# Two graph attention layers per graph: head outputs kept feature-major, score rows sent through DRAM

## The chip, the cores, the metric

One core of a Trainium2 chip runs the whole program: 32 graphs, one after the other, in one launch. The metric is device time in microseconds (us), the median over executions. Two kernels that are compared in rounds ran on the same chip.

In the profile PE is TensorE, PEld its weight load, DVE VectorE, ACT ScalarE, POOL GpSimd, SP the engine that only issues DMAs. SBUF is the large on-chip memory, PSUM the small one that TensorE writes into.

## The reference, cut to what matters

```python
def reference(x, adj, ...):            # x (32, 512, 512), adj (32, 512, 512)
    h = maximum(layernorm(x), 0)
    x = x + L0(h, adj)                 # one attention over the neighbours, values = h
    h = maximum(layernorm(x), 0)
    return x + L1(adj, h)              # two GAT layers: 4 heads x 256 features with elu, then 1 head x 512

# an attention, with s the sources and d the destinations:
#   e[s, d] = leaky_relu(a[s] + c[d], 0.2);  -inf where there is no edge
#   out[d]  = sum_s softmax_s(e)[s, d] * value[s]
```

A graph has three kinds of attention: layer 0, the four heads of the first GAT layer (layer 1 below), and the second GAT layer (layer 2). Both kernels compute E[s, d] = exp(leaky(a[s] + c[d]) - m[d]) with s on the partitions, m[d] being leaky(c[d] + the largest a[s] over d's neighbours). With p = c - m and q = 0.2 c - m this is exp(max(a + p, 0.2 a + q)). So three rows must lie on all 128 partitions: a for the maxima, p and q for the weights.

## The kernel before: the parts that matter

```python
def spread(col_of):                    # a value per node -> a row on all partitions, IN PSUM
    row = p_bc.tile([P, N], F32, tag="bc", name="row")
    for t in range(T):
        nc.tensor.transpose(row[:, node_block(t)], col_of(t).to_broadcast([P, P]), ident)
    return row

def neighbour_max(amax, h, mask, row):             # 4 instructions on VectorE
    ... nc.vector.tensor_tensor_reduce(junk, mask[:, t, :], row, 1.0, LOWEST, ALU.add, ALU.max, accum_out=...)

def edge_weights(E, pq, h, a_of, a2_of, mask):
    p_row = spread(...); q_row = spread(...)
    for t in range(T):
        nc.scalar.activation(q, q_row, AF.Identity, bias=a2_of(t), scale=1.0)                    # ScalarE
        nc.vector.scalar_tensor_tensor(u, p_row, a_of(t), q, op0=ALU.add, op1=ALU.max)           # VectorE: "u"
        nc.gpsimd.tensor_add(u, u, mask[:, t, :])                                                # GpSimd: mask add
        nc.scalar.activation(E[:, t, :], u, AF.Exp)                                              # ScalarE

def inverse_sums(E):                   # 16 matmuls with a column of ones
    ...
# ... (cut) a head: acc[d, f] = E^T x values, one column of ones behind the 256 features for the sum;
# normalise, add bias, elu on VectorE; then eight TensorE transposes to get the feature-major h1T.
# Masks are transposed by TensorE. TensorE's order is left to the scheduler.
```

## Time and profile before

| | before |
|---|---|
| median of 3 runs | 5194.93 us (5193.39 to 5204.31) |
| TensorE busy, records | 96%, 20,224 |
| VectorE, ScalarE, GpSimd busy | 45%, 34%, 21% |
| granted TensorE clock, mean | 0.931 |
| one graph, from one graph's hn transposes to the next's | 160.3 us |

The prediction below shows the lines behind this table. This is from the page of the kernel before; the columns are line, engine, operation, output<-inputs, shapes, count | busy us in all, mean ns of one | idle time before them:

```profile
L204 POOL TENSOR_TENSOR u<-u,m 128x512 f32<-128x512 f32 x640 | 737.8, 1180 | 1844.2 <-DVE u L203 1803.7
...
L203 DVE SCALAR_TENSOR_TENSOR u<-row,ac,q 128x512 f32<-128x512 f32 x640 | 447.5, 745 | 747.5 <-ACT q L201 746.1
...
L180 DVE CUSTOM_DVE_ANT_0 junk_m<-m1T,row 128x512 bf16<-128x512 bf16 x640 | 394.4, 683 | 124.9 <-PE row L165 124.9
```

The mask add takes 1180 ns, u 745 ns, a masked maximum 683 ns. In u and in the maximum one input (`row`) is in PSUM.

### The profile page before, as it was taken

The page shows a single profiled execution, that of the slowest core. Times are in us where ns is not written, and L with a number is a line of the kernel's source. Part 1 is how long each engine was busy: PE and PEld are TensorE (multiplying, and loading weights), DVE is VectorE, ACT ScalarE, POOL GpSimd, SP SyncE. Part 2 cuts the span into 40 slices and gives each one's busy share as a digit, 9 for nine tenths or more (in the row PEclk, how much of TensorE's full clock was granted, in tenths as well). Part 3 has the DMA queues.
Part 4 walks back from the last instruction along what each step waited for, and adds up shares of the span by engine and source line. Part 5 has one row for each costly group of instructions (what it writes and reads, how often), then busy time and mean ns, then how long its engine had stood idle before and what let it go on. Part 6 is the DMA issues. An engine that isn't in the chain of part 4 may idle for free.

```text
span 5205.4 us, 52686 instructions
## 1 busy us (share of the span) xinstructions
PE 5003.1 (96%) x20224; PEld 3228.5 (62%) x20224; DVE 2326.8 (45%) x6180; ACT 1794.5 (34%) x2945; POOL 1108.0 (21%) x998
## 2 busy tenths in 40 slices
PE   6999999999999999999999999999999999999999
PEld 3666656666566666666665666656666666666565
DVE  5454434454444544345443444444454434544343
ACT  2333323433224333233332333322433323333232
POOL 1222211222112212122221222211221212222121
PEclk8899999999999999999999999999999999999999
DMA  2000000000000000000000000000000000000000
GB/s 103 20 13 17 25 25 25 9 17 25 25 25 9 17 25 25 25 17 17 17 25 25 25 9 17 25 25 25 9 17 25 25 25 17 17 17 25 9 9 9
DMA packets 53802, 111.11 MB, mean 21 GB/s; under 512 B 1840, under 2 KB 1840, under 8 KB 53552
## 3 DMA queue, kind: packets, MB, share of 16 engines
q1 hardware_dynamic: 50688, 100.67, 5.5%
q10 hardware_dynamic: 2864, 7.08, 0.4%
q8 instruction: 160, 2.62, 0.2%
q14 instruction: 90, 0.74, 0.0%
HBM read 74.19 MB, written 33.55 MB: 21 GB/s over the span
## 4 chain that ended last, share of the span: by engine, by line
PE 86%; POOL 5%; DVE 5%; ACT 3%; issue 1%; DMA 1%; DVEq 0%; POOLq 0%; ACTq 0%; SPq 0%
PE acc L222 31%; PE acc L399 18%; PE acc L333 17%; PE ps_c L309 8%; POOL u L204 5%; PE row L165 4%; PE pt L173 3%; PE ps L212 3%; DVE u L203 3%; ACT q L201 2%; ACT E L205 1%; DVE v L367 1%; DMA x<-in_x_dram 0%; DVE junk L126 0%; DMA adj<-in_adj_dram 0%
## 5 line engine op out<-in xcount | busy, mean ns | idle before, releaser
L222 PE MATMUL acc<-xl,E 128*128 128x257 f32 (+1 forms) x5120 | 1548.6, 453 | 67.2 <-ACT E L205 62.1
L222 PEld LDWEIGHTS acc<-xl,E 128*128 128x128 f32 x5120 | 996.0, 203 | 470.4 <-issue 258.1
L204 POOL TENSOR_TENSOR u<-u,m 128x512 f32<-128x512 f32 x640 | 737.8, 1180 | 1844.2 <-DVE u L203 1803.7
L399 PE MATMUL acc<-w_s,h1T 128*128 128x512 f32 x2048 | 952.9, 619 | 0.0
L333 PE MATMUL acc<-w_s,hT 128*128 128x512 f32 x2048 | 917.3, 604 | 0.0
L203 DVE SCALAR_TENSOR_TENSOR u<-row,ac,q 128x512 f32<-128x512 f32 x640 | 447.5, 745 | 747.5 <-ACT q L201 746.1
L333 PEld LDWEIGHTS acc<-w_s,hT 128*128 128x128 f32 x2048 | 392.1, 196 | 449.8 <-issue 449.8
L399 PEld LDWEIGHTS acc<-w_s,h1T 128*128 128x128 f32 x2048 | 397.9, 201 | 436.7 <-issue 436.7
L201 ACT ACTIVATE q<-row,a 128x512 f32<-128x512 f32 x768 | 478.9, 682 | 535.2 <-PE row L165 428.4
L338 ACT COPY xl<-acc 128x512 f32<-128x512 f32 x256 | 150.1, 586 | 1340.7 <-PE acc L333 1340.7
L205 ACT ACTIVATE E<-u 128x512 f32<-128x512 f32 x768 | 484.2, 630 | 222.2 <-POOL u L204 221.2
L222 PE MATMUL acc<-h,E 128*128 128x512 f32 x1024 | 453.8, 601 | 6.0 <-DVE x L284 6.0
L180 DVE CUSTOM_DVE_ANT_0 junk_m<-m1T,row 128x512 bf16<-128x512 bf16 x640 | 394.4, 683 | 124.9 <-PE row L165 124.9
L309 PEld LDWEIGHTS ps_c<-wa,h1T 128*128 128x128 f32 x2048 | 335.4, 257 | 50.2 <-PE pt L173 34.1
L309 PE MATMUL ps_c<-wa,h1T 128*128 128x2 f32 x2048 | 333.1, 295 | 28.1 <-DVE r L216 28.1
L222 PEld LDWEIGHTS acc<-h,E 128*128 128x128 f32 x1024 | 194.7, 193 | 238.2 <-issue 224.1
L174 ACT COPY h1T<-pt 128x512 f32<-128x512 f32 x256 | 138.8, 581 | 551.3 <-PE pt L173 551.3
L411 DVE SCALAR_TENSOR_TENSOR x<-acc,r,x 128x512 f32<-128x512 f32 x128 | 96.1, 751 | 401.5 <-PE acc L222 401.5
L165 PE MATMUL row<-ident,pq 128*128 128x128 f32 x1536 | 210.6, 277 | 62.7 <-ACT q L201 53.3
L212 PEld LDWEIGHTS ps<-ones,E 128*128 128x128 f32 x2048 | 258.9, 198 | 11.2 <-ACT E L205 5.4
L212 PE MATMUL ps<-ones,E 128*128 128x1 f32 x2048 | 246.6, 246 | 4.4 <-ACT E L205 4.4
L165 PEld LDWEIGHTS row<-ident,pq 128*128 128x128 f32 x1536 | 175.3, 139 | 120.4 <-ACT q L201 71.1
(71 smaller groups left out, 3727.8 us busy)
## 6 DMA issues: line engine op xcount, KB each, us to landing
adj<-in_adj_dram SPq DMA_DIRECT2D x32, 1024.0 KB, 5.1
x<-in_x_dram SPq DMA_DIRECT2D x32, 1024.0 KB, 5.1
out_dram<-x SPq DMA_DIRECT2D x32, 1024.0 KB, 4.2
w_s<-in_L_gnn_W_dram ACTq DMA_DIRECT2D x2, 2048.0 KB, 21.1
b_r<-in_L_gnn_b_dram ACTq DMA_DIRECT2D x1, 512.0 KB, 11.2
a_r<-in_L_gnn_att_src_dram ACTq DMA_DIRECT2D x1, 512.0 KB, 5.4
a_r<-in_L_gnn_att_dst_dram ACTq DMA_DIRECT2D x1, 512.0 KB, 4.0
ws_r<-in_L_gnn_attn_w_src_dram ACTq DMA_DIRECT2D x1, 256.0 KB, 5.2
```

Of the source, the lines that this page charges most:

```text
L165: nc.tensor.transpose(row[:, node_block(t)], col_of(t).to_broadcast([P, P]), ident)
L173: nc.tensor.transpose(pt[:, node_block(t)], src(t, k), identity)
L180: nc.vector.tensor_tensor_reduce(junk, mask[:, t, :], row, 1.0, LOWEST, ALU.add, ALU.max, accum_out=amax[:, t, h : h + 1])
L201: nc.scalar.activation(q, q_row, AF.Identity, bias=a2_of(t), scale=1.0)
L203: nc.vector.scalar_tensor_tensor(u, p_row, a_of(t), q, op0=ALU.add, op1=ALU.max)
L204: nc.gpsimd.tensor_add(u, u, mask[:, t, :])
L205: nc.scalar.activation(E[:, t, :], u, AF.Exp)
L212: nc.tensor.matmul(ps[:, t : t + 1], E[:, s, node_block(t)], ones, start=(s == 0), stop=(s == T - 1))
L222: nc.tensor.matmul(acc[:, :width], E[:, s, node_block(t)], values(s), start=(s == 0), stop=(s == T - 1))
L309: nc.tensor.matmul(ps[:, t, :], src[:, k, node_block(t)], wa[:, k, :], start=(k == 0), stop=(k == kn - 1))
L333: nc.tensor.matmul(acc, hT[:, k, node_block(t)], w1_s[:, k, half * 512 : (half + 1) * 512], start=(k == 0), stop=(k == KD - 1),)
L399: nc.tensor.matmul(acc, h1T[:, k, node_block(t)], w2_s[:, k, :], start=(k == 0), stop=(k == KH - 1))
```

## The change

The intent is to take work from TensorE, which bounds the kernel. The heads are aggregated feature-major, so that their output needs no transposes; rows are spread by four small writes to DRAM and a broadcast read; masks are transposed by DMA; the four E tiles of an attention are added up on GpSimd, so that the softmax's sums need 4 matmuls in place of 16; the scores of the second GAT layer are dot products on VectorE; TensorE's instructions are pinned to program order. Its core (cuts marked by "..."):

```diff
+    def matmul(*args, **kwargs):
+        tc.keep_in_program_order(nc.tensor.matmul(*args, **kwargs))
 ...
-    def spread(col_of):
-        row = p_bc.tile([P, N], F32, tag="bc", name="row")
-        for t in range(T):
-            nc.tensor.transpose(row[:, node_block(t)], col_of(t).to_broadcast([P, P]), ident)
+    def to_dram(name: str, n: int):
+        nc.vector.transpose(turned, spots[name])
+        for q in range(0, P, 32):
+            nc.sync.dma_start(d[:, q : q + 32], turned[q : q + n * T, :])
+    def spread(d, first: int, n: int, tag: str, bufs: int):
+        r = work.tile([P, n, N], F32, tag=tag, name=f"r_{tag}", bufs=bufs)     # in SBUF
+        nc.sync.dma_start(r, src)                                              # src: broadcast to 128 partitions
 ...
     def edge_weights(...):
-            nc.vector.scalar_tensor_tensor(u, p_row, a_of(t), q, op0=ALU.add, op1=ALU.max)
+            nc.vector.scalar_tensor_tensor(u, pq_rows[:, 0, :], a[:, t : t + 1], u, op0=ALU.add, op1=ALU.max)
             nc.gpsimd.tensor_add(u, u, mask[:, t, :])
+        nc.gpsimd.tensor_add(total, E[0], E[1])
+        for e in E[2:]:
+            nc.gpsimd.tensor_add(total, total, e)
 ...
-        transposed(lambda t, k: m1[:, t, node_block(k)], m1T, ident_b, BF16)
+            nc.sync.dma_start_transpose(m1T[:, :, own], m1[:, t, :])
 ...
     def layer1_head(...):
+        for k in range(FK):
+            for s in range(T):
+                matmul(acc, xh[:, h, at : at + P], E[s], start=(s == 0), stop=(s == T - 1))
+        inverse_sums(total, spot(f"r{h % 2}")[:, :T])
+        r_row = spread(to_dram(f"r{h % 2}", 1), 0, 1, "r_row", 2)[:, 0, :]
+            nc.vector.tensor_mul(v, acc, r_row)
+            ...                                                                # elu, straight into xh
```

## The prediction

> **What bounds the kernel now.** I read five views, in this order.
>
> First the page's engine totals and the start of the chain of work that ended last:
>
> ```profile
> PE 5003.1 (96%) x20224; PEld 3228.5 (62%) x20224; DVE 2326.8 (45%) x6180; ACT 1794.5 (34%) x2945; POOL 1108.0 (21%) x998
> ...
> PE 86%; POOL 5%; DVE 5%; ACT 3%; issue 1%; DMA 1%; DVEq 0%; POOLq 0%; ACTq 0%; SPq 0%
> ```
>
> TensorE is busy nearly always and is 86% of the chain. So the time is the number of TensorE passes times their pace, plus the few places where it waits. A float32 matmul shows as two records (2048 records for 1024 matmuls of the second projection); I call each a pass.
>
> Second, the timeline of TensorE, which gives the period and the pace. The transposes of hn come once per graph, first at about 82 us, then:
>
> ```profile
> 231.47 1.04 PE L173 MATMUL pt<-ident,hn 128*128 128x128 f32 x8
> ```
> ```profile
> 5040.76 1.04 PE L173 MATMUL pt<-ident,hn 128*128 128x128 f32 x8
> ```
>
> That is 30 graphs in 4809.3 us: 160.3 us a graph. From 5040.8 to the end (5205.4) are 164.6 us. So: 82 at the start, 150 for the first graph, 30 times 160.3, 165 at the end.
>
> The pace is the distance from one row's start to the next row's, over the first row's count:
>
> ```profile
> 2615.06 22.48 PE L399 MATMUL acc<-w_s,h1T 128*128 128x512 f32 x52
> 2637.38 1.04 PE L173 MATMUL pt<-ident,hn 128*128 128x128 f32 x8
> 2638.25 3.41 PE L212 MATMUL ps<-ones,E 128*128 128x1 f32 x30
> 2641.52 1.47 PE L173 MATMUL pt<-ident,hn 128*128 128x128 f32 x8
> ...
> 2733.33 8.91 PE L222 MATMUL acc<-xl,E 128*128 128x257 f32 x40
> 2742.08 1.04 PE L173 MATMUL pt<-ident,v 128*128 128x128 f32 x8
> ...
> 2759.09 8.88 PE L309 MATMUL ps_c<-wa,h1T 128*128 128x2 f32 x52
> 2767.84 2.06 PE L399 MATMUL acc<-w_s,h1T 128*128 128x512 f32 x2
> ```
>
> 512 columns: 22.32/52 = 0.429 us a pass. 257 columns: 8.75/40 = 0.219. One column: 3.27/30 = 0.109, the same as a float32 transpose (0.87/8 = 0.109), although it does almost nothing: a weight load is paid in full. The scores of the second attention: 8.75/52 = 0.168. The bfloat16 mask transposes run at 0.073 (8 in 0.58 us).
>
> Third, busy time by stretch, which shows why 0.168 and not 0.109:
>
> ```profile
> core 0: us, PE busy (x) PEld busy (x) DVE busy (x) ACT busy (x) POOL busy (x), PEclk, DMA share, GB/s
> 231.47:391.80 160.33, 155.50 (x633) 100.77 (x632) 71.86 (x190) 56.03 (x92) 34.58 (x31) 0.94 0.06 20
> 2759.10:2767.80 8.70, 8.70 (x53) 8.70 (x52) 0.32 (x2) 2.93 (x4) 6.71 (x6) 0.64 0.01 2
> ```
>
> The granted clock is 0.94 over a graph but 0.64 in that run of two-column matmuls, and TensorE idles 4.8 us a graph.
>
> Fourth, what each group of instructions costs (the list of groups, used below). Fifth, the timeline near 43 us, for what the change newly lays on VectorE and GpSimd:
>
> ```profile
> 41.43 4.86 POOL L204 TENSOR_TENSOR u<-u,m0T 128x512 f32<-128x512 f32 x4 [21.66 <-DVE u L203]
> ...
> 43.91 1.36 DVE L126 SCALAR_TENSOR_TENSOR junk<-w_s,a_r 128x256 f32<-128x256 f32 x1
> ...
> 45.20 1.37 DVE L126 SCALAR_TENSOR_TENSOR junk<-w_s,a_r 128x256 f32<-128x256 f32 x1
> ...
> 46.50 0.41 DVE L126 SCALAR_TENSOR_TENSOR junk<-w_s,a_r 128x256 f32<-128x256 f32 x1
> ```
>
> The same VectorE instruction takes 1.36 us while a GpSimd add runs and 0.41 us once the adds are over. Four GpSimd adds with three such instructions between them took 4.86 us, elsewhere 4.50.
>
> **What the Trainium skill says.** "SBUF — State Buffer", section "SBUF: two separate sides": VectorE and GpSimd share a port pair that is an exclusive lock, taken by a GpSimd instruction or by a VectorE instruction in a two-port mode or with two SBUF inputs. The rows above agree. In the kernel before, the two heavy VectorE steps (u, 745 ns x24 a graph; masked maximum, 683 ns x24) read their row from PSUM, so only one input is in SBUF, and u indeed keeps 732 to 759 ns beside GpSimd.
>
> "TensorE: Matmul & The Clock Gate", Part 1: the clock is gated down when the array was little busy. The 0.64 agrees.
>
> "DMA: Bandwidth & Descriptors", "Anatomy of one DMA": about 2 us fixed per DMA, mostly completion. The nearest here is a 256 KB row broadcast, 3.2 us at its fastest, and 512 KB, 4.0 us.
>
> **The change part by part, per graph.**
>
> *TensorE now, at full pace:* 192 passes of 512 (82.4 us), 128 of 257 (28.0), 72 row transposes (7.8), 32 mask transposes (2.3), 48 transposes of v and hn (5.2), 64 sum passes (7.0), scores 32 at 0.109 and 64 at 0.168 (14.2). Sum 146.9. The measured 160.3 has 13.4 more: 4.8 idle, the rest a lowered clock and slow restarts.
>
> *Removed:* rows 7.8, masks 2.3, transposes of v 3.5 (the head's output comes feature-major), scores of the second attention 10.8, and 16 of the 64 sum passes 1.7 (layer 0 and layer 2 go from 32 each to 8 each; each of the four heads gains 8 in place of the ones column). Heads: 128 passes of 257 become 64 of 512, 28.0 to 27.5. Together 26.6.
>
> *TensorE after:* 256 passes of 512 (109.9), 16 transposes (1.7), 32 score passes (3.5), 48 sum passes (5.2): 120.3 us. The fixed order is: turn and scores 5.2, project 27.5, layer 2 out of the graph before 14.6, four heads 31.0, layer 0 out of the next graph 14.6, second projection 27.5. Each wait is meant to be covered by an unrelated block.
>
> *Rows through DRAM:* 11 round trips a graph. Each is a VectorE turn (estimate 0.2), four small writes whose issue takes 0.37 to 0.45 each on the SP queue (its rows of before) plus about 2 to land, then a broadcast read of 3 to 4. Estimate 7.5 us, in place of a transpose that was there within 1 us.
>
> *VectorE:* it loses the normalisation of v (242.6), the reciprocals (79.9), the elu (157.9 + 101.8): 18 us a graph. It gains 8 products with r at 0.75, 8 clamps at about 0.4, 8 maxima at 0.68 (15) and 8 dot products at 0.77 (6), plus 11 turns. 72.7 becomes about 78.
>
> *GpSimd:* it keeps 34.6 and gains 18 adds of two float32 tiles; the one like it (x plus b2) takes 1270 ns: +22.9, to 57.5.
>
> *ScalarE:* loses eight copies of h1T and eight of masks (about 9 us), 56 to about 47. Not a bound.
>
> *The shared port:* now u, the maxima, the dots and the elu all have both inputs in SBUF. Data time of a 512-wide one: estimate 0.53, twice the 0.27 by which the 512-wide dot (680 ns) exceeds the 256-wide one (414). 24 u + 24 maxima + 16 dots + 8 elu maxima = 72 of 0.53, with clamps and masks about 6: 44 us. GpSimd: 46 adds at about 1.0 to 1.1: 50. Together 94 of 120 us.
>
> *Where it can end up on the path.* One set of edge weights costs 4 x (1.125 + 0.39) + 3 x 1.27 = 9.8 us of that port. (A 256-wide VectorE instruction added 0.36/3 = 0.12 to GpSimd; a 512-wide one has 0.27 more.) Count from the end of the second projection. Layer 2's edges end near 30: dots 2, round trip 7, maxima 3, shifts 0.8, round trip 7.7, edges 9.8. TensorE needs them at 33 (turn, scores, project), so this just fits. From 30 on the port owes five sets, 49 us, and some 9 us of elu and of the next graph's masks and dots before layer 0's edges are ready: near 88. TensorE arrives there at 33 + 14.6 + 31 = 78.6. Estimate: a wait of up to 9 us a graph, less if VectorE fills earlier gaps, more if queues in order block each other.
>
> **Sum.** 120.3, plus 9 for waits and clock: 129 us a graph. Start about 90 (two round trips and DMA transposes against TensorE turns, but 16 fewer weight folds). End about 164: the last graph has no layer 0 to fill with, but saves passes, and its layer 2 chain of 30 us lies open. 90 + 31 x 129 + 164 = 4253. I say 4250.
>
> **The rivals.**
>
> *TensorE stays the only bound.* The waits are covered and the clock rises because the long run of two-column matmuls is gone. 122.5 us a graph, about 4050. For it: 62% PEld and a clock of 1.00 in the stretches of 512-wide passes. Against: 94 us of port in a chain with only 13 E buffers.
>
> *VectorE and GpSimd take over as bound,* each stretched by the other. 138 to 145 us a graph, 4530 to 4750. For it: 1.36 against 0.41 us. Against: the sum is still below TensorE's.
>
> *The DRAM round trips come onto the path.* Head 3's reciprocal needs 7.5 us plus the elu before the second projection can finish, with 14.6 us of layer 0 out to cover it; layer 2's edges have two trips in 33 us. If SP's in-order queue holds reads behind a late write, add 5 to 10 us a graph: 4400 to 4560. DMA bandwidth is no rival: 22 rows of 256 KB and 3 MB of data a graph are 8.9 MB in 129 us, 69 GB/s, and the kernel reached 252 GB/s in its first 50 us.
>
> *The saving does not appear* (same or slower): it would need over 35 us of waits a graph. Nothing in the counts gives that.
>
> **Range and chances.** 122.5 us a graph gives the low side, 138 the high: 4070 to 4520. Faster by over 2%: 0.95; within 2%: 0.03; slower: 0.02. The chances of a slowdown are those of queue blocking that I cannot see from here.
>
> **What would show it.** Right: 352 passes a graph in place of 632, so 11,264 TensorE records in place of 20,224; period near 129, clock above 0.94, u and maxima with means clearly above 0.7 us and maxima of 1.5 us, TensorE waiting on GpSimd's sums or on E at layer 0 out and layer 2 out. Wrong: TensorE under 85% busy (a rival took over), VectorE's means unchanged (the lock does not matter), or large waits that end in a DMA of r, pq or a.

## The result, and the profile after

| | before | after |
|---|---|---|
| median us | 5199.39 (4 runs, 5193.39 to 5204.31) | 5534.19 (4 runs, 5533.43 to 5534.92) |
| ratio | 1 | 1.0648 (95% interval 1.0633 to 1.0663) |
| granted clock | 0.931 | 0.867 |
| one graph | 160.3 us | 171.0 us |

The ratio is the mean time of one kernel's fast runs over that of the other's of the same rounds, so it is not quite the ratio of the medians quoted. The kernel became 6.5% slower. The prediction was 4250 us, 18% faster, with a range of 4070 to 4520: the direction was wrong, and not only the size.

The page of the changed kernel, engine totals and the start of the chain of work that ended last:

```profile
PE 4406.6 (80%) x11264; PEld 2094.2 (38%) x11264; DVE 3367.7 (61%) x6956; ACT 1604.4 (29%) x2561; POOL 2204.0 (40%) x1542
...
PE 46%; DVE 22%; POOL 15%; issue 6%; DMA 5%; ACT 4%; SPq 1%; DVEq 0%; POOLq 0%; ACTq 0%
```

The records are the 11,264 predicted: the passes did go. But TensorE is busy 80% of the time, not 96%, and only 46% of the chain is on it. VectorE (22%) and GpSimd (15%) took its place.

The timeline of TensorE over one graph, cut to the two hn transposes that bound the period and to the long waits (start, us, instructions, and in brackets the wait before them and what ended it):

```profile
2621.23 1.04 PE L87 MATMUL pt<-ident,hn 128*128 128x128 f32 x8
...
2680.13 9.46 PE L84 MATMUL acc_T<-E,xh 128*128 128x512 f32 x16 [7.11 <-ACT E L219]
...
2703.10 1.84 PE L84 MATMUL ps<-ones,total 128*128 128x1 f32 x8 [3.23 <-DVE spot_r L232]
...
2721.34 5.91 PE L84 MATMUL acc_T<-E,xh 128*128 128x512 f32 x8 [10.91 <-DVE v L398]
...
2747.07 1.87 PE L84 MATMUL ps<-ones,total 128*128 128x1 f32 x8 [11.27 <-POOL total L224]
...
2792.22 1.04 PE L87 MATMUL pt<-ident,hn 128*128 128x128 f32 x8
```

The period is 2792.22 - 2621.23 = 171.0 us. The four long waits shown are 7.1 us for the first head's E, 3.2 for the reciprocal of the sums (without which the next sums have no bank), 10.9 for v, which must empty the accumulators of an earlier head, and 11.3 for the sums that GpSimd pre-adds for layer 0. With five short ones that are cut here all waits come to 34 us a graph. The predicted passes at full pace were 120.3. What is left, 171.0 - 34 - 120.3 = 17 us, is put down here to a lowered clock and slow restarts (an estimate: it is a remainder, not a measurement). The clock does vary inside this graph: 0.76 in the 9.9 us after the wait of 7.1 us, 1.00 in the second projection at the end.

The same graph by engine, in the view of busy time by stretch:

```profile
core 0: us, PE busy (x) PEld busy (x) DVE busy (x) ACT busy (x) POOL busy (x), PEclk, DMA share, GB/s
2621.23:2792.22 170.99, 136.63 (x353) 64.96 (x352) 104.15 (x215) 50.10 (x80) 69.08 (x48) 0.87 0.21 59
```

VectorE is busy for 104 us (predicted 78), GpSimd for 69 (predicted 57.5). Why is in the groups, to be held against those of before:

```profile
L217 POOL TENSOR_TENSOR u<-u,m 128x512 f32<-128x512 f32 x640 | 937.6, 1486 | 2047.2 <-DVE u L216 2047.2
...
L216 DVE SCALAR_TENSOR_TENSOR u<-r_rows,spot_a,u 128x512 f32<-128x512 f32 x768 | 972.4, 1316 | 670.2 <-ACT u L215 661.6
...
L196 DVE CUSTOM_DVE_ANT_0 junk_m<-m1T,r_row 128x512 bf16<-128x512 bf16 x640 | 564.7, 929 | 46.1 <-DMA r_row<-d_a 45.9
```

The mask add went from 1180 to 1486 ns, u from 745 to 1316, the maximum from 683 to 929 (layer 0's, which fall beside GpSimd's pre-adds, to 1634). None of these three does more work than before. What changed for u and the maximum is that their row is in SBUF.

The timeline of all engines at one place shows the mechanism. The three pre-adds of an attention stand beside VectorE's masked maxima:

```profile
2653.01 1.71 POOL L222 TENSOR_TENSOR total<-E,E 128x512 f32<-128x512 f32 x1
...
2654.80 3.27 POOL L224 TENSOR_TENSOR total<-total,E 128x512 f32<-128x512 f32 x2
...
2655.21 1.75 DVE L196 CUSTOM_DVE_ANT_0 junk_m<-m1T,r_row 128x512 bf16<-128x512 bf16 x1
...
2658.56 0.68 DVE L196 CUSTOM_DVE_ANT_0 junk_m<-m1T,r_row 128x512 bf16<-128x512 bf16 x1
```

The same instruction takes 1.75 us while GpSimd adds, and 0.68 us as soon as the adds have ended. A tiny instruction shows it even more plainly: the [128x4] product that scales layer 0's a (one input, once a graph) takes 1.09 us at the median and 0.125 at the fastest. The Trainium skill ("SBUF — State Buffer", section "Who interferes with whom") says that `tensor_scalar` can enter the modes that take the shared pair; this trace agrees: one such product began at 2695.21, after the start of a pre-add on GpSimd, and ended at 2696.30, with the pre-add (2696.27).

Last, VectorE just before the 10.9 us wait for v:

```profile
2713.82 0.17 DVE L232 RECIPROCAL spot_r<-ps 128x4 f32<-128x4 f32 x1
...
2715.61 1.74 DVE L196 CUSTOM_DVE_ANT_0 junk_m<-m,r_row 128x512 bf16<-128x512 bf16 x1
...
2718.94 1.74 DVE L196 CUSTOM_DVE_ANT_0 junk_m<-m,r_row 128x512 bf16<-128x512 bf16 x1
...
2720.61 1.28 DVE L398 TENSOR_TENSOR v<-acc_T,r_r_row 128x512 f32<-128x512 f32 x2
```

The four masked maxima of the next graph's layer 0 stand ahead of v in VectorE's order. They take 1.5 to 1.7 us each beside GpSimd's adds. But they are only part of the 10.9 us, for v also needs its row of reciprocals, `r_r_row`, and that was late. The SP queue shows it: the writes of head 0's r, a write of head 1's r, and only then the read of head 0's:

```profile
2703.23 1.26 SPq L160 DMA_DIRECT2D d_r<-turned_r  x4
...
2714.26 0.24 SPq L160 DMA_DIRECT2D d_r<-turned_r  x1
2714.67 0.34 SPq L166 DMA_DIRECT2D r_r_row<-d_r  x1
```

The read came 10.2 us after the last of its own writes (2704.49 to 2714.67). It stood behind one write for head 1, which had to wait until VectorE turned head 1's r at 2714.02. The reads of the other three heads came within 2 us of their writes. In run 13 below such a read took 3.3 us from issue to use (2510.60 to 2513.87), so v could not have begun here before about 2717.9 (an estimate); the maxima account for the last 2.7 us or so. So two things delay v: stretched instructions ahead of it, and a read that stands in order behind an issue that waits.

### The profile page after: what moved, and what is told of

Its sections match the earlier page's. It is cut to its first block, busy times and chain, and to the rows that moved or that the text cites. A ratio compares the mean times of both kernels' runs of the same rounds, so it can differ in the third digit from the quotient of the medians.

```text
span 5532.2 us, 39813 instructions
## 1 busy us (share of the span) xinstructions
PE 4406.6 (80%) x11264; PEld 2094.2 (38%) x11264; DVE 3367.7 (61%) x6956; ACT 1604.4 (29%) x2561; POOL 2204.0 (40%) x1542
## 4 chain that ended last, share of the span: by engine, by line
PE 46%; DVE 22%; POOL 15%; issue 6%; DMA 5%; ACT 4%; SPq 1%; DVEq 0%; POOLq 0%; ACTq 0%
PE acc L84 35%; DVE junk_m L196 10%; POOL u L217 10%; PE acc_T L84 6%; DVE u L216 6%; POOL total L224 4%; ACT u L215 2%; PE ps_c L84 2%; DMA r_row<-d_a 2%; DVE junk L190 2%; PE ps L84 2%; DMA adj<-in_adj_dram 2%; POOL total L222 1%; DMA r_rows<-d_pq 1%; ACT hT L324 1%
## 5 line engine op out<-in xcount | busy, mean ns | idle before, releaser
L217 POOL TENSOR_TENSOR u<-u,m 128x512 f32<-128x512 f32 x640 | 937.6, 1486 | 2047.2 <-DVE u L216 2047.2
L84 PE MATMUL acc_T<-E,xh 128*128 128x512 f32 x2048 | 1180.3, 729 | 552.9 <-DVE v L398 321.8
L216 DVE SCALAR_TENSOR_TENSOR u<-r_rows,spot_a,u 128x512 f32<-128x512 f32 x768 | 972.4, 1316 | 670.2 <-ACT u L215 661.6
L84 PEld LDWEIGHTS acc_T<-E,xh 128*128 128x128 f32 x2048 | 453.8, 233 | 1202.9 <-ACT E L219 423.3
L84 PE MATMUL acc<-w_s,xh 128*128 128x512 f32 x2048 | 886.5, 593 | 3.7 <-DVE xh L402 3.7
L215 ACT ACTIVATE u<-r_rows,a 128x512 f32<-128x512 f32 x768 | 505.8, 711 | 784.9 <-DMA r_rows<-d_pq 536.7
L196 DVE CUSTOM_DVE_ANT_0 junk_m<-m1T,r_row 128x512 bf16<-128x512 bf16 x640 | 564.7, 929 | 46.1 <-DMA r_row<-d_a 45.9
L84 PEld LDWEIGHTS acc<-w_s,xh 128*128 128x128 f32 x2048 | 389.5, 190 | 494.8 <-issue 489.5
L224 POOL TENSOR_TENSOR total<-total,E 128x512 f32<-128x512 f32 x384 | 562.5, 1465 | 22.6
L84 PEld LDWEIGHTS ps<-ones,total 128*128 128x128 f32 x1536 | 241.2, 235 | 647.7 <-POOL total L224 488.1
L84 PE MATMUL acc<-xl,E 128*128 128x512 f32 x1024 | 449.6, 597 | 0.0
```

Of the source, the lines that this page charges most:

```text
L84: tc.keep_in_program_order(nc.tensor.matmul(*args, **kwargs))
L215: nc.scalar.activation(u, pq_rows[:, 1, :], AF.Identity, bias=a2[:, t : t + 1], scale=1.0)
L216: nc.vector.scalar_tensor_tensor(u, pq_rows[:, 0, :], a[:, t : t + 1], u, op0=ALU.add, op1=ALU.max)
L224: nc.gpsimd.tensor_add(total, total, e)
```

## The experiments

There were eighteen runs, of seventeen kernels (runs 16 and 17 are the same one). In the expectations L stands for the theory of the lock (both VectorE inputs in SBUF, so u and the maxima alternate with GpSimd), Q for that of the round trips through DRAM and of queues that hold them up, O for the order of instructions alone, W for the wait of the maxima for their row. The kernel before took 5180 to 5208 us in the same sessions.

### 1. Rows in PSUM, on purpose with wrong contents

```diff
+    flat = p_row.tile([P, N], F32, tag="flat", name="flat"); nc.vector.memset(flat, 0.0)   # one PSUM bank
+        tick = cols.tile([P, 1], F32, ...); nc.vector.tensor_copy(tick, row[:, 0:1])       # keeps the DMA used
-                junk, mask[:, t, :], row, 1.0, ...
+                junk, mask[:, t, :], flat, 1.0, ...
-            nc.vector.scalar_tensor_tensor(u, pq_rows[:, 0, :], ...)
+            nc.vector.scalar_tensor_tensor(u, flat, ...)
```

> Changed kernel, but u and the masked maximum read a constant row in PSUM in place of the broadcast row in SBUF (wrong result on purpose; one VectorE copy of a column keeps the wait for the broadcast; one transpose bank fewer). So neither has two SBUF inputs. Theory L (the port that VectorE and GpSimd share stretches both and so delays the edge weights): u falls from 1316 to about 745 ns, the maxima to about 690, GpSimd's mask add from 1486 to about 1200, and the time from 5530 to about 4600, because TensorE's 34 us of waits a graph fall to under 15. Theory Q (trips through DRAM and queues in order hold things up): the same shorter instructions, but the waits for r_rows and for the reciprocal row stay, time 5200 to 5400.

Measured: 4693.0 us, 841 less than the changed kernel. (It computes from a constant row; its output stayed within the tolerance all the same, which means nothing.) The group of u:

```profile
L216 DVE SCALAR_TENSOR_TENSOR u<-flat,spot_a,u 128x512 f32<-128x512 f32 x768 | 546.3, 746 | 518.9 <-ACT u L215 502.4 <-POOL total L224 16.4
```

u is back at 746 ns, the maxima at 678, the mask add at 1158, a graph at 143.6 us. This looked like the lock alone. It was not quite, as runs 9 and 13 show: the tick waits for the row's DMA, but the maxima no longer do.

### 2. No pre-adds

```diff
-        nc.gpsimd.tensor_add(total, E[0], E[1]) ... (3 adds)
+        total = total_1                               # a constant tile
```

> Changed kernel without the 18 GpSimd pre-adds a graph: the sums are taken of a constant tile (wrong result on purpose). Theory L with the pre-adds as the larger part of GpSimd's share: the 11 us wait before layer 0's sums goes, the maxima fall from 929 towards 700 ns, time 4700 to 4900. Theory Q: only the wait for the sums goes, time about 5200 or more.

Measured: 4813.5 us, 721 less. u stays at 1214 ns, since the mask adds remain, and the maxima of layers 1 and 2 fall to 774. So the adds are a large part of the loss. They can cost as work in series with the sums and as load on the shared port; this run does not separate the two.

### 3. r without DRAM

```diff
-        inverse_sums(total, spot(...)[:, :T]); r_row = spread(to_dram(...), ...)
+        ps = p_sm.tile([P, N], F32, ...); matmul(ps, ones_sq, total, start=True, stop=True)
+        r_row = work.tile([P, N], F32, ...); nc.vector.reciprocal(r_row, ps)
```

> Changed kernel, but a head's sums come by one matmul of a square of ones with the pre-added tile, so broadcast over the partitions in PSUM, and the reciprocal is taken of that: no trip through DRAM for r (right result). TensorE's passes of 512 columns take about the same 0.9 us as eight of one column. Theory Q: the 10.9 us wait of the third head for a PSUM buffer and the 3.2 us wait for the sums' bank go, 14 us and the slow clock after them: time 4900 to 5050. Theory L: VectorE is held by stretched maxima at that place anyway, time 5350 to 5550.

Measured: 5659.9 us, 126 more; a miss. The reciprocal of a whole [128x512] row took 3346 ns on VectorE, four times a graph, where the trip needed one of [128x4]. The run says that VectorE is scarce; it does not tell what r's trip costs.

### 4. TensorE's order left free

```diff
-        tc.keep_in_program_order(nc.tensor.matmul(*args, **kwargs))
+        nc.tensor.matmul(*args, **kwargs)
```

> Changed kernel with TensorE's order left to the scheduler, the one part of the change undone that needs no other edit. If the fixed order is what makes TensorE stand (other passes could fill the waits): under 5200. If waits for u, E and rows bound the period whatever the order, or if the fixed order helps: within 2% of 5534 or above it.

Measured: 5359.5 us, correct. The fixed order costs 175 us, 3%, as things stand; without it the kernel is still slower than before.

### 5 and 6. Only u, only the maxima, from PSUM

Run 1's edit, first for u alone, then for the maxima alone.

> Only u reads the constant row in PSUM; the maxima keep their row in SBUF (wrong result on purpose). If the lock theory holds and the edge weights are the chain that counts: u back to about 745 ns, GpSimd's mask add to about 1200, and well over half of the 841 us that the first such run gained: 4900 to 5100. If the order the scheduler chose made that gain and not the port: the split between this run and the next says nothing about instruction times, and this one may stay near 5500.

> Only the masked maxima read the constant row in PSUM; u keeps its row in SBUF (wrong result on purpose). Lock theory: maxima at 690 ns, u still at 1200 or more, time 5150 to 5350; the gains of this run and of the one before add up to about 841 us, or to more if either alone would free the same waits.

Measured: 5194.6 us (-340; result wrong) and 4891.5 us (-643). The two add to 983, more than run 1's 841. The second was far better than expected. With hindsight a likely reason is that the maxima's edit also frees them from waiting for their row, which u's edit does not do (u still waits for the q row through ScalarE). It was not shown by these two runs, whose orders were not held equal.

### 7. Rows in PSUM and no pre-adds

Runs 1 and 2 together.

> Both rows in PSUM and no pre-adds (wrong result on purpose): nearly no contention for the port is left. Against 120.3 us of TensorE passes a graph this shows what the trips through DRAM, queues in order and the clock cost by themselves. Lock theory: 4200 to 4350, TensorE over 95% busy. If trips and queues matter much too: over 4450 with TensorE waiting on rows from DRAM.

Measured: 4245.2 us, clock 0.958, TensorE 96% busy, 129.8 us a graph. That is the predicted 129 and 4250. So TensorE's passes were predicted rightly, and the rest is small once VectorE and GpSimd do not get in the way and the maxima need not wait. That the rest fits to a microsecond is partly luck: the 9 us of the prediction were to be mostly a wait for the shared port, but in this run TensorE waits only some 3 us a graph, and the other 6.6 (129.8 - 120.3 - 2.9) are pace and clock.

### 8. Rows copied to PSUM by ScalarE (correct)

```diff
+        p_row_ = p_row.tile([P, N], F32, tag="prow", ...); nc.scalar.copy(p_row_, pq_rows[:, 0, :])
+        a_row = p_row.tile([P, N], F32, tag="prow", ...); nc.scalar.copy(a_row, row)
```

> A right result without the lock on u and the maxima: ScalarE copies each a row and each p row from SBUF into PSUM (12 copies of about 0.6 us a graph; the turn's PSUM tiles come from the accumulators' pool so that two banks are free). Lock theory: close to the run with constant rows, 4650 to 4850, so faster than both kernels. Theory that the added ScalarE step lies on the chain: 4900 to 5200.

Measured: 5117.4 us. The durations were those of run 1 (u 745, maxima 679), the time was 424 us longer: a miss. Something other than durations had gone into run 1.

### 9 and 10. The same order, only the row's place changed

Run 1 and run 8 differ in instruction order too. So the next kernel was scheduled twice: once as run 1, to record the order of every engine, then with `flat` in SBUF and that order forced by edges that set an order and no wait. Run 10 does the same to run 7. The order of all five engines was compared and is equal.

```diff
-    p_row = ctx.enter_context(tc.tile_pool(name="p_row", bufs=1, space=PSUM))
+    p_row = ctx.enter_context(tc.tile_pool(name="p_row", bufs=1))               # SBUF
```

> The PSUM-row experiment (4693 us) with one difference: its constant row lies in SBUF. Every engine keeps the instruction order of that experiment, forced with edges of order only, so schedule and DMA traffic are the same. Theory L (lock on the shared port when both VectorE inputs are in SBUF): u back to 1200 to 1350 ns, maxima to 900 to 1600, mask add to 1450, time 5250 to 5550. Theory O (the PSUM experiment gained by its order, the bank or the added tick copy): u may lengthen, but the time stays within 3% of 4693.

Measured: 5221.6 us against run 1's 4693.0. The place of one constant row, with the same order, the same DMAs and the same arithmetic, costs 529 us. The groups of VectorE in it:

```profile
L216 DVE SCALAR_TENSOR_TENSOR u<-flat,spot_a,u 128x512 f32<-128x512 f32 x768 | 900.7, 1213 | 491.1 <-ACT u L215 473.8 <-POOL total L224 16.5
...
L196 DVE CUSTOM_DVE_ANT_0 junk_m<-m,flat 128x512 bf16<-128x512 bf16 x128 | 203.8, 1627 | 0.0
```

u is at 1213 and layer 0's maxima are at 1627 ns. The time is a little below the expected range, and 313 us below the changed kernel: the lock is shown, but it is not all.

> The same change on the experiment that had both rows in PSUM and no pre-adds (4245 us): only the row's place moves, to SBUF, with that experiment's order on every engine. Theory L: with the pre-adds gone GpSimd still holds the port for the mask adds, so u near 1200 and maxima 770 to 900 ns, and 4650 to 4850 us as in the run without pre-adds alone (4813). Theory O: within 3% of 4245.

Measured: 4471.0 us, against 4245.2. Its output is wrong, which doesn't matter for the time. With only the mask adds on GpSimd the lock costs 226 us, about half of the 405 to 605 that were expected: a miss in size. The other 303 of the 529 us appear only when the pre-adds are there too (and with them another order).

### 11. Rows copied to PSUM by VectorE (correct)

Run 8 with `nc.vector.tensor_copy` in place of `nc.scalar.copy`.

> Correct kernel: VectorE itself copies the a and p rows from SBUF into PSUM (12 copies of 128x512 a graph), then reads them there. Theory L with no other limit: u 745 and maxima 680 ns, each copy 0.4 to 0.8 us (7 us of VectorE a graph), 4700 to 4900 us. If the ScalarE copies' loss (5117 us) came from where the row's bank sits in the order and not from ScalarE's queue, this stays at 5000 to 5150 too.

Measured: 5155.7 us, maxima at 680 ns; a miss like run 8, and so not ScalarE's queue.

### 12. Rows turned by TensorE again, the pinned order kept (correct)

```diff
+    def pe_row(col_of):
+        row = p_row.tile([P, N], F32, tag="prow", name="row")
+        [nc.tensor.transpose(row[:, node_block(t)], col_of(t).to_broadcast([P, P]), ident) for t in range(T)]
+        return row
-        neighbour_max(amax, 0, m0, spread(a_d, 0, 1, "row", 2)[:, 0, :])
+        neighbour_max(amax, 0, m0, pe_row(lambda t: a[:, t : t + 1]))      # the same for all a, p and q rows
```

> Correct kernel: the a, p and q rows are made as before the change, by four TensorE transposes each into a PSUM bank (free in order among the ordered matmuls); only r still goes through DRAM. Undoes the 'rows through DRAM' part alone. Theory L: u 745, maxima 680 ns; TensorE has 72 x 0.109 = 7.8 us more a graph than the PSUM-row experiment (143.4 us a graph) but no round trips: 4750 to 4950 us. If the lock is not the cause and round trips were: also faster, but u and maxima would stay long.

Measured: 5431.3 us, with u at 745 and the maxima at 682 ns: a miss. (The edit also took the accumulators from five banks to four.) TensorE's waits name the main reason:

```profile
PE row L169 <- DVE spot_pq L208: 250.0, 31, 8.9
```

The turns themselves were not pinned, but each matmul was pinned behind whatever TensorE instruction stands before it in the program, and that may be a turn whose input is late. Waits on rows came to some 550 us in all. An undo under a fixed order does not undo one thing.

### 13 and 14. The maxima's wait put back, with the row in PSUM and in SBUF

```diff
+            reduce_i = nc.vector.tensor_tensor_reduce(junk, mask[:, t, :], flat, ...)
+            after(tc, reduce_i, tick_i)       # the maxima come behind the tick, which waits for the row's DMA
```

> The PSUM-row experiment (4693 us) in which the masked maxima also wait for their row's round trip through DRAM, as in the changed kernel (there they read a constant and only a side copy waited). Theory W (the 312 us left over are the wait for the a row, 10 us a graph): 4950 to 5150 us, with the extra time as waits on layer 0's sums and on VectorE's later results. Theory O (they are instruction order): 4650 to 4800.

> The run above with one difference: its constant row lies in SBUF, same instruction order on every engine, same waits. The lock's share once more: 400 to 550 us over the run above. Against the changed kernel (5534) it differs in order (and the side copies) alone: under W 5400 to 5600, under O about 5220, as the same-order SBUF run without the wait.

Measured: 5103.6 us with the row in PSUM and 5562.0 in SBUF, at one and the same order. The four runs set the place of the row against the wait:

| time, us | row in SBUF | row in PSUM | the lock |
|---|---|---|---|
| maxima wait for their row | 5562.0 | 5103.6 | 458 |
| maxima do not wait | 5221.6 | 4693.0 | 529 |
| the wait, with its order | 340 | 411 | |

Within a row of the table the order is equal on all engines; between the rows it is not. The changed kernel itself, 5534, lies 0.5% from the 5562 of the same two conditions at another order (and with the side copies), so order alone made little difference there. Theory O fell in its plain form, which forecast 4650 to 4800 and about 5220. L is shown, twice, at equal order. W is shown only together with the order that the scheduler chose with the wait; a run with run 13's order and without the wait is missing. Runs 8 and 11, which remove the lock and keep the wait, now fit: 5117 and 5156 against 5104.

Where the wait arises is seen in the run of 5103.6 us. First the SP queue, with the issue of layer 0's a row to DRAM, of a head's r, and of the read of a:

```profile
2494.90 1.28 SPq L162 DMA_DIRECT2D d_a<-turned_a  x4
2501.13 1.25 SPq L162 DMA_DIRECT2D d_r<-turned_r  x4
2502.55 0.34 SPq L168 DMA_DIRECT2D r_row<-d_a  x1
...
2509.85 0.58 SPq L162 DMA_DIRECT2D d_r<-turned_r  x2
2510.60 0.34 SPq L168 DMA_DIRECT2D r_r_row<-d_r  x1
```

The last two lines are the next head's first writes and then the read of the first head's r: as in the changed kernel, it comes long after its own writes (8.2 us), because it stands behind writes that wait. In runs 1 and 9, where the maxima need not wait, these reads come 0.9 to 1.8 us after their writes. So the wait and the late read of r came together, and no run here separates them.

Now VectorE, the tick and the first maximum behind it:

```profile
2509.75 0.11 DVE L195 COPY tick<-r_row 128x1 f32<-128x1 f32 x1
2509.78 0.68 DVE L198 CUSTOM_DVE_ANT_0 junk_m<-m,flat 128x512 bf16<-128x512 bf16 x1
```

a leaves VectorE at 2494.9 and its row is used at 2509.8, 14.9 us later; I had estimated 7.5. The read was issued only at 2502.55, behind the writes of r, which waited until 2501.13 for VectorE to turn r. A little later in the same queue a read of r followed its last write's end of issue by 1.87 us (2511.64 to 2513.51), so by the same distance a's read could have been issued near 2498 (an estimate). The rest, up to 2509.8, is the landing and VectorE's own order: it had u to finish first, and at 2509.78 the maxima did not stand still for the DMA. The Trainium skill ("DMA: Bandwidth & Descriptors", section "Anatomy of one DMA") says that a wait on a semaphore happens on the issuing sequencer, before dispatch; here the issue that waits holds up the one behind it, which did not depend on it. TensorE's waits for layer 0's sums and for v are longer in this run. With the wait (line numbers are two higher in this kernel):

```profile
PE ps L86 <- POOL total L226: 407.8, 34, 71.9
PE acc_T L86 <- DVE v L400: 280.4, 33, 9.5
```

and in run 1, without it:

```profile
PE ps L84 <- POOL total L224: 261.8, 33, 62.7
PE acc_T L84 <- DVE v L398: 73.8, 31, 2.7
```

Together 688 us against 336.

### 15. ScalarE's copies with TensorE's order free (correct)

Run 8 with run 4's edit.

> Correct: ScalarE copies the a and p rows to PSUM (5117 us with the fixed order) and TensorE's order is left to the scheduler. Freeing the order gained 175 us in the changed kernel as it was: 4900 to 5050 if waits on layer 0's sums can be filled with other passes; 5100 or more if the queues in order on VectorE and GpSimd are what is late.

Measured: 5117.0 us, the same as with the fixed order; a miss. The scheduler's order found nothing to put into these waits; why it did in run 4 and not here was not looked into.

### 16. Rows turned by TensorE, order free (correct)

Run 12 with run 4's edit.

> Correct: a, p and q rows turned by TensorE, no DRAM trip but for r, TensorE's order left to the scheduler (5431 us with matmuls pinned behind the turns that stand before them in the program, 443 us of it waits on those turns). TensorE has 128 us of passes a graph at full pace; with the waits filled 135 to 150 us a graph: 4450 to 4900 us. If freeing gives no more than the 175 us it gave before: 5250.

Measured: 4633.2 us, clock 0.963. This removes both causes, the row in SBUF and the wait for its trip, by undoing one part of the change (and the pinned order).

### 17 and 18. Timed, and one bank moved (correct)

```diff
-    p_acc = ... bufs=4 ...;  p_row = ... bufs=3 ...
+    p_acc = ... bufs=5 ...;  p_row = ... bufs=2 ...
```

> The same kernel as the run of 4633 us (a, p and q rows turned by TensorE into PSUM, TensorE's order free), timed: 4600 to 4660 us, ratio to the kernel before 0.885 to 0.90, interval within 0.5%.

> The same with five accumulator banks and two row banks in place of four and three. If the waits on v (201 us, 6.5 us a graph) come from too few accumulator banks: 4450 to 4560. If they come from r's trip itself, or two row banks hold the turns back instead: 4600 to 4800.

Measured, with 4 runs each against 7 of the kernel before (median 5197.54 us): run 16's kernel again 4651.31 us, ratio 0.8954 (95% interval 0.8934 to 0.8975); with the bank moved 4488.15 us (4459.35 to 4492.44), ratio 0.8623 (0.8593 to 0.8653). The line of run 17 that the fifth bank removed:

```profile
PE acc L84 <- DVE v L398: 140.8, 31, 6.1
```

Run 18 has 0.6 us of this wait. Its page:

```profile
PE 4255.1 (95%) x13568; PEld 2176.5 (49%) x13568; DVE 2601.5 (58%) x6732; ACT 1578.1 (35%) x2561; POOL 1864.3 (42%) x1542
...
PE 76%; POOL 11%; DVE 6%; ACT 3%; issue 2%; DMA 1%; SPq 0%; POOLq 0%; DVEq 0%; ACTq 0%
```

Run 18 beats both kernels: 13.8% below the kernel before. Feature-major heads, DMA transposes of masks, pre-adds and dot products stay; the a, p and q rows go back to TensorE and PSUM, and only r goes through DRAM.

## Why the prediction was wrong, point by point

*TensorE's passes* (120.3 us a graph): right. 11,264 records were predicted and found, and run 7 reached the predicted period and time.

*The shared port*: seen, and right in kind. Predicted was that u and the maxima would grow clearly above 0.7 us; they grew to 1.32 and 0.93. A set of edge weights was put at 9.8 us of the port; in the trace the mask adds and pre-adds of one set run from 2646.76 to 2658.07, 11.3 us. That is 15% off, or some 9 us over a graph's six sets (an estimate), far from the 42 us between 129 and 171.

*What failed* is the step from there: "Together 94 of 120 us", and "a wait of up to 9 us a graph, less if VectorE fills earlier gaps, more if queues in order block each other". It treated the port as a resource of its own that is free 26 us a graph. But an instruction that waits for the port also holds its engine, and with it all that stands behind it in that engine's order. VectorE was put at 78 us a graph; it was held for 104. Of the difference, 24 u at 0.57 us more than before (13.7) and 24 maxima (20 at 0.25, 4 at 0.95 more: 8.8) are 22.5. What TensorE waits for (v, the reciprocals, the next row) stands in that queue. So the wait of up to 9 us became 34 us of waits, beside the lowered clock. The lock alone decides the sign: with the same waits and the row in PSUM (run 13) the kernel takes 5104 us, against 5189 for the kernel before in that session (one look each; 1.6%, twice the spread of repeats), and with the row in SBUF 5562. In its place the runs showed these steps, as periods of one graph:

| | us a graph | step |
|---|---|---|
| changed kernel | 171.0 | |
| same waits, row in SBUF (run 14) | 170.6 | 0.4 |
| row in PSUM, same order (run 13) | 157.0 | 13.6, the lock |
| maxima no longer wait for their row (run 1) | 143.6 | 13.4, the maxima's wait for their row, with the order that came with it (r's late read included) |
| no pre-adds (run 7) | 129.8 | 13.8, GpSimd's pre-adds in the way of the sums, with a change of order |
| predicted | 129 | |

The sizes depend on what is taken away first: without pre-adds the lock is worth 226 us rather than 529.

*The round trips*: named as a rival, with the cause that the trace shows (a read held behind a late write: 10.2 us after its own writes for r in the changed kernel, 6.4 for a and 8.2 for r in run 13), at 5 to 10 us a graph. Run 13 against run 1 has the wait at 13.4, the change of order included. But the rival was given as an alternative to the port, when it came on top of it.

*VectorE and GpSimd as bound*: the rival nearest to the truth, at 138 to 145 us a graph. It lacked the waits for rows, and the clock.

*The clock*: predicted above 0.94, found 0.867. The remainder over passes and waits was 17 us a graph; run 7, with only some 3 us of waits, still has 6.6 of it, so about 10 can go with the long waits (an estimate). In the runs whose waits were short (7, 16, 18) the clock was 0.958 to 0.974. That the waits lower the clock is read from this pairing and was not tested by itself.

*Its own sign of being wrong* was met: it gave TensorE under 85% busy, and 80% was found. *Its range* did not follow from its working at the low end: 90 + 31 x 122.5 + 164 is 4052, not 4070.

*The saving does not appear*: called out of reach because "it would need over 35 us of waits a graph. Nothing in the counts gives that". It needed waits and clock together, 51 us over the passes, and counts could not give it: only the order of the engines' queues could. A chance of 0.02 for slower was too sure for a change that moves eleven dependent round trips a graph into in-order queues.

What stays open: how much of the 13.4 us is the maxima's wait and how much the order that came with it, r's late read above all; how much is the landing of a row and how much the queue in front of it (no run put the reads on a queue of their own); and what r's and q's trips cost by themselves.

## What to carry to other kernels

When work is moved from a full engine to idle ones, ask in which memory its operands will lie: a VectorE instruction with two SBUF inputs alternates with GpSimd, and one with its row in PSUM does not (u here: 1213 against 746 ns at the same order). Count not only busy time but what stands in order behind an instruction or an issue that waits. Where an experiment takes a wait away along with the thing that it tests, as run 1 did, build the pair that differs in one of the two before believing it.

## What the Trainium skill lacked or had wrong

- "SBUF — State Buffer", "Who interferes with whom": it lists copies, casts, `tensor_scalar` and `tensor_tensor` among those that meet GpSimd. Its rule (two SBUF inputs) holds for two more that it does not name: the masked maximum (`tensor_tensor_reduce`, layer 0's, beside pre-adds, 666 to 1627 ns when its row moves from PSUM to SBUF at the same order) and `scalar_tensor_tensor` (u, 746 to 1213 ns at the same order).
- The same page, section "SBUF: two separate sides", gives a full block for the whole instruction. A mask add (1158 ns) and a u (746 ns) that alternate came every 1.57 us, not every 1.90 us (four mask adds in 6.28 us from 2677.82 in the changed kernel, u's beside all of them): part of their times overlaps.
- The same page says nothing of short instructions: a [128x4] `tensor_scalar` took 1.09 us beside GpSimd against 0.12 us.
- "VectorE: DVE Perf Modes", "First, the fixed hardware budget": it says that a reciprocal repeats, but gives no duration. A [128x512] float32 reciprocal took 3.35 us, about four and a half times u's 0.75.
- "DMA: Bandwidth & Descriptors", "Anatomy of one DMA": about 2 us for one DMA, in a section on DMAs that GpSimd issues; the kernel here issues from SP. A chain of four small writes and a broadcast read on one issuing queue took 14.9 us from the end of the value to its use, 7.7 of them until the read was issued, and the last part behind other work in VectorE's order. No page looked at here counts such a chain.
